# Gated cross-attention block: evictions of the VO stage shared out, exponentials of the first softmax spread, sums of the first attention reordered

## The chip, the core and the metric

The kernel runs on one core of a Trainium2 chip. The core has five engines that run side by side, each with its own in-order queue: TensorE (PE in the profile, with PEld for its weight loads) multiplies matrices into PSUM banks; VectorE (DVE) and ScalarE (ACT) work elementwise and can read PSUM; GpSimd (POOL) works elementwise on SBUF; SyncE (SP) issues DMAs. An instruction starts when those before it in its queue are issued and the semaphores that it waits for have been raised. The metric is the device time of one execution in microseconds (us), of which several runs are taken; the profiler's span is from the first to the last instruction of one execution.

## The reference, cut to what matters

All data is float32: `x` is (4, 2048, 512), the context (4, 77, 384), 16 heads of 64, a softmax over 77 keys.

```python
def attention(x, context, Wq, Wk, Wv, Wo, bo):
    q, k, v = split_heads(x @ Wq), split_heads(context @ Wk), split_heads(context @ Wv)
    attn = softmax(einsum('bhid,bhjd->bhij', q, k) * 64 ** -0.5)
    return merge_heads(einsum('bhij,bhjd->bhid', attn, v)) @ Wo + bo

def ffn(x, W, b, logits, u):                      # one of 8 weight matrices, by a gumbel draw
    idx = argmax(log_softmax(logits) - log(-log(u)))
    return x @ W[idx] + b[idx]

x = x + tanh(g_xattn) * attention(layernorm(x), ctx_768, Wq, Wk, Wv, Wo, bo)
x = x + tanh(g_ffn) * ffn(layernorm(x), W, b, logits, u)
```

## The kernel before

**Folded weights.** The queries and the output projection are folded into the small context once per batch: M = Wq K^T, so that scores are `x M`, and VO = V Wo for each head, so that attention's output is `P VO`. The keys are padded to 80 and laid out as ten chunks of 128 rows (8 keys of each of the 16 heads); `tgx`, the gate tanh(g_xattn), is multiplied into VO when it leaves PSUM.

**Groups.** The 8192 tokens are worked in 16 groups of 512. For each group `i` there are three products: scores (`ps_s`), attention (`ps_a`) and feed-forward (`ps_f`). Work of neighbouring groups is interleaved by hand: the schedule is the order of the Python statements (`tc.manual_schedule()`), and each engine runs its instructions in that order. Nothing is planned by costs.

**Seven products for eight.** Class `Seven` multiplies 2x2 blocks with seven block products (Strassen's method in Winograd's form). The sums of column blocks (T1 to T4, `Columns.sum`) and of weight blocks (`weight_sum`) are made on GpSimd ahead. The order of the steps is in `ORDER`: (weight block, column block, accumulator, opens a bank).

```python
ORDER = ((0, "B11", 0, True), (3, "T1", 1, True), (4, "T2", 0, False), (1, "B21", 2, True),
         (5, "T3", 0, False), (6, "B22", 1, False), (2, "T4", 0, False))
```

Accumulators are used again: steps 0, 2, 4 and 6 all add onto accumulator 0, and after each of them `post(s)` reads the running sum out of PSUM. So step 2 may start only when `post(0)` has read, step 4 after `post(2)`, step 6 after `post(4)`. `post` of steps 0, 1, 2 and 6 is a copy on ScalarE (L472, for attention with a bias at L476); `post` of steps 3, 4 and 5 is an addition on VectorE (L491). Weight sums: `weight_sum(w, 0)` makes block 5, 1 makes block 3, 2 makes block 4, 3 makes block 6 (L123). Attention's second step therefore needs `weight_sum(vo, 1)` and T1 of the probabilities, its third `weight_sum(vo, 2)` and T2. The scores of a group come as three `Seven`s: `s0` (two row blocks), `s1` (two) and `s2` (one); `s1` and `s2` run together in a loop of seven steps.

**Softmax of a group.** Scores are transposed on VectorE into the tile `s` (`s_rows`, L520), four heads' parts side by side (16 token slices each). `head_max` (VectorE, L529 and L531) gives a negative scaled maximum, `exps(i, a, b)` runs exponentials number a to b-1 out of 64 (ScalarE, L537, one for each token slice of a head part), `head_sum` adds rows and takes the reciprocal (VectorE, L544 and L545), `head_scale` multiplies (GpSimd, L548), and `p_columns(i, k0, k1)` transposes chunks k0 to k1-1 of the result into `pT` (VectorE, L557); each chunk takes a part of all four head parts. `pT` chunks 0 to 4 are the upper half and feed T1. The tile `s` exists once: the scores of the next group overwrite it.

**The stretch around the change** (L738 to L800) lies between the first group's scores and its attention. It holds the building of VO for head pairs 3 to 7 (`build_vo`: six matmuls into six banks, six evictions with the gate, L339 on VectorE or L341 on ScalarE as the letters of its argument say in turn, then four stores to DRAM), the scores of group 1, and the softmax of group 0. `load_vo(0)` fetches VO back in its blocked form after the last store. `centre_wf` and `weight_sum(wf, ..)` prepare the feed-forward weight on GpSimd. Seven PSUM banks rotate among all products. After that a loop over the groups begins at L802; in its first pass (i = 1) attention of group 0 runs beside the softmax of group 1, with T2, T3, T4 of the probabilities and `weight_sum(vo, 3)` on GpSimd, and then the feed-forward of group 0, whose T1 is made on GpSimd from attention's last residuals (L924 to L929).

Of the kernel before, what the change touches and what calls it, by code (L numbers as in the profile page):

```python
# [19 lines left out]
def flamingo_block_kernel(  # L20
# [34 lines left out]
    NT, D = x.shape  # L55
# [32 lines left out]
    def bank(name):  # L88
        return pm.tile([P, 512], F32, tag="mm", name=name)
# [8 lines left out]
    vo = cp.tile([P, 7, KH, D // 2], F32, tag="vo")  # L98
# [8 lines left out]
    def pieces(t, at, n):  # L107

        return [t[:, ds(at + e * n * T, n * T)].rearrange("p (n v t) -> p n v t", v=2, t=T2) for e in range(2)]
# [4 lines left out]
    def flat(t):  # L114
        n = len(t.shape) - 1
        names = " ".join("abcdef"[:n])
        return t.rearrange(f"p {names} -> p ({names})")

    def weight_sum(w, n, engine=None):

        to, a, b_, op = ((5, 0, 3, ALU.subtract), (3, 3, 2, ALU.add), (4, 3, 0, ALU.subtract),
                         (6, 1, 4, ALU.subtract))[n]
        (engine or nc.gpsimd).tensor_tensor(flat(w[:, to]), flat(w[:, a]), flat(w[:, b_]), op)  # L123
# [65 lines left out]
    def by_chunk(t):  # L189

        return t.rearrange("p (a q e) -> p q a e", a=NA, e=32)

    def chunked(t):
        return t.rearrange("p (q a e) -> p q a e", a=NA, e=32)
# [61 lines left out]
    def v_cols(p, at, n):  # L256
        return vT_f[:, ds(p * BP + at, n)] if p < 7 else wf_f[:, ds(6 * D + at, n)]
# [65 lines left out]
    def stage_of(h):  # L323

        return vo_st[h if h < 2 else 2 + (h - 2) % (len(vo_st) - 2)]

    def build_vo(p, engines):
        n = 0
        for c in range(3):
            r = min(P, BP - c * P)  # L330
            for hh in range(2):
                stg = stage_of(2 * p + hh)
                hr = ts(hh, DH)
                ps = bank("ps_vo")

                nc.tensor.matmul(ps, v_cols(p, c * P, P)[hr], wo[hr, p, :], start=True, stop=True)  # L336
                src, dst = by_chunk(ps[:r, :]), chunked(stg[:r, c, :])
                if engines[n % len(engines)] == "D":
                    nc.vector.tensor_scalar(dst, src, tgx[:r], None, ALU.mult)  # L339
                else:  # L340
                    nc.scalar.activation(dst, src, AF.Copy, scale=tgx[:r])  # L341
                n += 1
        for hh in range(2):
            d, stg = vo_d[2 * p + hh], stage_of(2 * p + hh)
            nc.sync.dma_start(out=d[0 : 2 * P].rearrange("(c r) e -> r c e", r=P), in_=stg[:, 0:2])
            nc.sync.dma_start(out=d[2 * P :], in_=stg[: BP - 2 * P, 2])
# [5 lines left out]
    def load_vo(bi):  # L352
        src = vo_d.rearrange("h (r b k) e -> (h r) b k e", b=B, k=NK)[:, bi]
        for o, c in ((0, 0), (1, 0), (1, 1), (0, 1)):
            nc.sync.dma_start(out=vo[:, BLK[o, c]], in_=src[:, ts(c, KH), ts(o, D // 2)])
# [63 lines left out]
    def key_chunk(t, k):  # L419

        return t.rearrange("p h g j -> p g h j")[:, :, :, ts(k, R)]
# [95 lines left out]
    def s_rows(i, k, cols):  # L517
        if i not in sc:
            sc[i] = wp.tile([P, HA, NG, JP], F32, tag="s", name="s")
        nc.vector.transpose(key_chunk(sc[i], k), cols.rearrange("p (g h r) -> p g h r", h=HA, r=R))  # L520

    def head(i, h):
        return sc[i][:, h, :, :J]
# [3 lines left out]
    def head_max(i, h):  # L527
        mx = stat[:, ds((16 + h) * NG, NG)]
        nc.vector.tensor_reduce(mx, head(i, h), AX.X, ALU.max)  # L529
        nmx[h] = small.tile([P, NG], F32, tag=f"nmx{h}", name="nmx")  # L530
        nc.vector.tensor_tensor(nmx[h], mx, norms[i].down, ALU.mult)  # L531

    def exps(i, n0, n1):

        for n in range(n0, n1):
            h, g = n // NG, n % NG
            nc.scalar.activation(head(i, h)[:, g, :], head(i, h)[:, g, :], AF.Exp,  # L537
                                 scale=norms[i].up[:, g : g + 1], bias=nmx[h][:, g : g + 1])
# [3 lines left out]
    def head_sum(i, h):  # L542
        sums[h] = sm = small.tile([P, NG], F32, tag=f"sm{h}", name="sm")
        nc.vector.tensor_reduce(sm, head(i, h), AX.X, ALU.add)  # L544
        nc.vector.reciprocal(sm, sm)  # L545

    def head_scale(i, h):
        nc.gpsimd.tensor_tensor(head(i, h), head(i, h), sums[h].unsqueeze(2).to_broadcast([P, NG, J]),  # L548
                                ALU.mult)

    def p_columns(i, k0, k1):
        for k in range(k0, k1):
            if k == 0:
                t = wp.tile([P, NK * T + KH * T2], F32, tag="pT", name="pT")
                pT[i] = Columns(t[:, : NK * T].rearrange("p (n t) -> p n t", t=T),
                                T1=t[:, NK * T :].rearrange("p (n t) -> p n t", t=T2))
            nc.vector.transpose(pT[i].all[:, k, :].rearrange("p (g h r) -> p g h r", h=HA, r=R),  # L557
                                key_chunk(sc[i], k))
# [103 lines left out]
    def centre_wf(wfr, c):  # L662
        nc.gpsimd.tensor_tensor(wfr[:, c, :], wfr[:, c, :], wf_mean, ALU.subtract)
        for o in range(2):
            nc.gpsimd.tensor_scalar(chunked(wf[:, BLK[o, c // 2], c % 2, :]), by_chunk(wfr[:, c, :])[:, ts(o, 2)],
                                    tgf, None, ALU.mult)
# [10 lines left out]
    def norm_step(n, s):  # L677
        if s == 0:
            n.gather()
        elif s == 1:  # L680
            n.calc()
            n.power()
        elif s == 2:
            n.back()
# [11 lines left out]
    s1 = Seven("ps_s", w_scores, xc[0], (2, 3), SNAP)  # L696
# [27 lines left out]
    s2 = Seven("ps_s", w_scores, xc[0], (4,), SNAP1)  # L724
# [15 lines left out]
    s1 = Seven("ps_s", w_scores, xc[1], (2, 3), pieces(spare, 0, 2))  # L740
    s2 = Seven("ps_s", w_scores, xc[1], (4,), SNAP1)
    head_max(0, 0)
    build_vo(3, "AAD")
    head_max(0, 1)
    exps(0, 0, 8)
    e = (8, 16, 24, 32, 41, 50, 57)
    for s in range(6):
        s0.product(s)
        s0.post(s)
        if s < 2:  # L750
            centre_wf(wfr, 2 * s)
            centre_wf(wfr, 2 * s + 1)
        if s == 2:
            weight_sum(wf, 0)
            weight_sum(wf, 1)
        if s == 3:
            weight_sum(wf, 2)
        if s < 4:
            build_vo(4 + s, "DDA" if s < 2 else "D")
        if s < 2:  # L760
            head_max(0, 2 + s)
        exps(0, e[s], e[s + 1])
        if s == 3:
            weight_sum(wf, 3)
            load_vo(0)
        if 3 <= s:
            head_sum(0, s - 3)
            head_scale(0, s - 3)
    exps(0, 57, 64)
    for s in range(7):  # L770
        s1.product(s)
        s2.product(s)
        if s == 0:
            s1.post(0)
            s2.post(0)
            s0.product(6)
            s0.post(6)
            head_sum(0, 3)
            head_scale(0, 3)
        if s == 3:  # L780
            norm_step(n1, 2)
        if 1 <= s < 5:
            p_columns(0, (0, 2, 5, 7)[s - 1], (2, 5, 7, 10)[s - 1])
        if s == 2:
            pT[0].sum("T1")
        if s == 3:
            weight_sum(vo, 0)
        if s == 4:
            weight_sum(vo, 1)
        if s == 5:  # L790
            weight_sum(vo, 2)
            for k in range(4):
                s_rows(1, (0, 1, KH, KH + 1)[k], s0.chunk(k // 2, k % 2))
        if 0 < s:
            s1.post(s)
            s2.post(s)
    for sv, k0, nk in ((s1, 2, 2), (s2, 4, 1)):
        for half in range(2):
            for k in range(nk):
# [2 lines left out]
    for i in range(1, NGRP):  # L802
# [4 lines left out]
        if 1 < i:  # L807
# [27 lines left out]
            s1 = Seven("ps_s", w_scores, xc[i], (2, 3), SNAP)  # L835
            s2 = Seven("ps_s", w_scores, xc[i], (4,), SNAP1)
# [35 lines left out]
        for s in range(7):  # L872
# [12 lines left out]
            if 1 <= s:  # L885
                e = (0, 10, 20, 32, 44, 56, 64)
# [225 lines left out]
```

## Time and profile before

| | us |
|---|---|
| median of 3 runs | 1246.3 (1245.36 to 1249.04) |
| the profiled execution: device time | 1246.03 |
| the profiled execution: span | 1244.2 |
| TensorE busy in it | 1234.0 (99%) |
| VectorE, GpSimd, ScalarE busy | 907.3 (73%), 895.4 (72%), 683.4 (55%) |
| VO pairs 3 to 7 with five score steps | 89.30 to 111.66 |
| the other score steps of group 1 | 111.66 to 135.17 |
| attention of group 0 | 135.17 to 165.39 |

The granted clock of TensorE was 0.998. Times in the profile count from the start of the span. A timeline row gives start, duration, engine, line, operation, output and inputs, shape and count of a run of like instructions, and in brackets the idle time ahead and what ended it. The chain that ended last is followed back from the last instruction; its rows give start, duration and what ran. In the waits, the columns are the total, the count and the longest wait.

### The profile page before, as it was taken

To read this page: it belongs to the slowest core of one execution; us is meant where nothing else is said; L and a number is where in the kernel's file an instruction comes from. 1 tells how busy PE (TensorE), PEld (TensorE's weight loads), DVE (VectorE), ACT (ScalarE), POOL (GpSimd) and SP (SyncE) were. 2 spreads that over 40 slices of the span, in tenths; PEclk is the share of its full clock that TensorE was granted. 3 is DMA by queue.
4 is the path that set the end of the run, shared out by engine and by line. 5 is a ranking of instruction groups with operands and counts; after the bars stand their busy time and mean duration, and the time that the engine had idled before them with its cause. 6 is when DMAs were issued, how large, how long until landed. Compare 5 with 4: busy or idle time off the path is not lost.

```text
span 1244.2 us, 16997 instructions
## 1 busy us (share of the span) xinstructions
PE 1234.0 (99%) x5704; PEld 1063.7 (85%) x5704; DVE 907.3 (73%) x1850; ACT 683.4 (55%) x1957; POOL 895.4 (72%) x486
## 2 busy tenths in 40 slices
PE   9999999999999999999999999999999999999997
PEld 6686888888888888888888888888888888888886
DVE  6778976666977766677776767776776877666576
ACT  4639545638274563827356382745638274563824
POOL 5558885857957785685968778575976877585766
PEclk9999999999999999999999999999999999999999
DMA  9868200314024030304106030212304121010102
GB/s 268 300 203 274 57 1 1 68 43 111 1 50 103 1 68 1 68 22 112 20 1 153 1 68 2 47 22 85 68 1 111 43 51 18 1 35 1 35 1 67
DMA packets 95221, 80.27 MB, mean 65 GB/s; under 512 B 3856, under 2 KB 83088, under 8 KB 95136
## 3 DMA queue, kind: packets, MB, share of 16 engines
q1 hardware_dynamic: 92496, 76.61, 24.1%
q10 hardware_dynamic: 2032, 1.47, 0.4%
q8 instruction: 45, 0.74, 0.3%
q0 software_dynamic: 608, 1.13, 0.2%
q14 instruction: 40, 0.33, 0.1%
HBM read 44.07 MB, written 35.13 MB: 64 GB/s over the span
## 4 chain that ended last, share of the span: by engine, by line
PE 96%; DVE 2%; ACT 0%; POOL 0%; issue 0%; DVEq 0%
PE ps_s L466 39%; PE ps_a L466 37%; PE ps_f L466 15%; PE ps_kv L270 2%; PE ps_vo L336 2%; PE ps_m L300 1%; DVE s L370 1%; PE ps_w L167 0%; ACT t L591 0%; POOL r L398 0%; DVE t L417 0%; DVE r L393 0%; DVE y L417 0%; DVE snap L491 0%; DVE y L587 0%
## 5 line engine op out<-in xcount | busy, mean ns | idle before, releaser
L466 PE MATMUL ps_a<-pT,vo 128*128 128x256 f32 x2240 | 486.2, 379 | 0.0
L466 PEld LDWEIGHTS ps_a<-pT,vo 128*128 128x128 f32 x2240 | 425.6, 190 | 57.9
L537 ACT ACTIVATE s<-s,nmx,up 128x77 f32<-128x77 f32 x1024 | 355.6, 445 | 0.8 <-DVE nmx L531 0.8
L437 POOL TENSOR_TENSOR pT<-pT 128x1280 f32<-128x1280 f32 x64 | 186.0, 2907 | 171.4 <-PE ps_a L466 161.9
L466 PE MATMUL ps_s<-tq,m 128*128 128x256 f32 x1280 | 290.6, 380 | 0.0
L466 PEld LDWEIGHTS ps_s<-tq,m 128*128 128x128 f32 x1280 | 242.6, 190 | 36.1 <-issue 2.3
L472 ACT COPY snap<-ps_s 128x512 f32<-128x512 f32 (+1 forms) x188 | 93.6, 515 | 292.7 <-DVE t L417 130.5
L466 PE MATMUL ps_s<-xc,m 128*128 128x256 f32 x960 | 221.1, 379 | 0.0
L466 PEld LDWEIGHTS ps_s<-xc,m 128*128 128x128 f32 x960 | 182.2, 190 | 27.3 <-issue 1.2
L548 POOL TENSOR_TENSOR s<-s,sm 128x1232 f32<-128x1232 f32 x64 | 145.2, 2271 | 46.7 <-DVE sm L545 46.7
L491 DVE TENSOR_TENSOR snap<-snap,ps_s 128x512 f32<-128x512 f32 (+1 forms) x141 | 83.7, 594 | 130.1 <-PE ps_s L466 125.0
L466 PE MATMUL ps_f<-tq,wf 128*128 128x256 f32 x512 | 118.3, 379 | 0.0
L557 DVE STREAM_TRANSPOSE pT<-s 128x512 f32<-128x512 f32 x160 | 101.0, 678 | 15.6 <-POOL s L548 15.6
L437 POOL TENSOR_TENSOR tq<-xc,tq 128x512 f32<-128x512 f32 x64 | 85.4, 1335 | 35.5 <-PE ps_f L466 33.0
L398 POOL TENSOR_TENSOR r<-r,neghalf 32x16 f32<-32x16 f32 (+1 forms) x33 | 93.2, 2833 | 21.9 <-DVE r L393 21.3
L466 PEld LDWEIGHTS ps_f<-tq,wf 128*128 128x128 f32 x512 | 97.3, 190 | 13.2
L544 DVE TENSOR_REDUCE sm<-s 128x16 f32<-128x1232 f32 x64 | 91.5, 1430 | 20.7 <-ACT s L537 20.7
L520 DVE STREAM_TRANSPOSE s<-snap 128x512 f32<-128x512 f32 x156 | 99.9, 685 | 6.1 <-ACT snap L472 3.8
L529 DVE TENSOR_REDUCE ps_st<-s 128x16 f32<-128x1232 f32 x64 | 92.4, 1444 | 2.1
L466 PE MATMUL ps_f<-xc,wf 128*128 128x256 f32 x384 | 90.7, 379 | 0.0
L437 POOL TENSOR_TENSOR tq<-xc 128x512 f32<-128x512 f32 x64 | 81.6, 1275 | 7.1 <-DVE xc L412 5.8
L472 ACT COPY snap<-ps_f 128x512 f32<-128x512 f32 x63 | 36.9, 586 | 87.8 <-PE ps_f L466 85.2
(138 smaller groups left out, 1187.0 us busy)
## 6 DMA issues: line engine op xcount, KB each, us to landing
xg<-in_x_dram SPq DMA_DIRECT2D x64, 256.0 KB, 6.0
out_dram<-y SPq DMA_DIRECT2D x60, 256.0 KB, 4.1
vo<-vo_d SPq DMA_DIRECT2D x16, 640.0 KB, 6.4
m<-m_d SPq DMA_DIRECT2D x12, 640.0 KB, 4.2
vo_d<-vo SPq DMA_DIRECT2D x14, 512.0 KB, 3.3
m_d<-vo SPq DMA_DIRECT2D x4, 960.0 KB, 5.0
wq<-in_WqT_dram SPq DMA_DIRECT2D x8, 256.0 KB, 6.5
wq<-in_Wo_dram SPq DMA_DIRECT2D x1, 2048.0 KB, 13.8
```

Of the source, the lines that this page charges most:

```text
L270: nc.tensor.matmul(ps[:, :n], w[:, c, ts(p, P)], keys[:, c].rearrange("p b j -> p (b j)"), start=(c == 0), stop=(c == NCC - 1))
L398: nc.gpsimd.tensor_tensor(r, r, neghalf[:32, : r.shape[1]], ALU.pow)
L437: (engine or nc.gpsimd).tensor_tensor(self.at[name], self.at[a], self.at[b_], op)
L466: nc.tensor.matmul(self.ps[r][:, n, :], self.w(blk, c, pair), self.cols(cname, c), start=(first and n == 0 and c == 0), stop=(c == h - 1), ...
L472: nc.scalar.copy(dst, self.ps[r])
L491: nc.vector.tensor_tensor(c, c, self.ps[r], ALU.add)
L520: nc.vector.transpose(key_chunk(sc[i], k), cols.rearrange("p (g h r) -> p g h r", h=HA, r=R))
L529: nc.vector.tensor_reduce(mx, head(i, h), AX.X, ALU.max)
L537: nc.scalar.activation(head(i, h)[:, g, :], head(i, h)[:, g, :], AF.Exp, scale=norms[i].up[:, g : g + 1], bias=nmx[h][:, g : g + 1])
L544: nc.vector.tensor_reduce(sm, head(i, h), AX.X, ALU.add)
L548: nc.gpsimd.tensor_tensor(head(i, h), head(i, h), sums[h].unsqueeze(2).to_broadcast([P, NG, J]), ALU.mult)
L557: nc.vector.transpose(pT[i].all[:, k, :].rearrange("p (g h r) -> p g h r", h=HA, r=R), key_chunk(sc[i], k))
```

## The change

The change touches only the order and the engine of instructions; what is computed stays the same.

- `build_vo` of pairs 4 to 7 takes the letters `ADD` (ScalarE, VectorE, VectorE in turn) in place of `DDA` for pairs 4 and 5 and `D` for pairs 6 and 7.
- Six exponentials in place of eight run before the loop over the `s0` steps, five to seven instead of seven to nine in each step, four after it; the last sixteen move into steps 0 to 3 of the `s1`/`s2` loop, four in each.
- `head_sum` and `head_scale` of head part 0 stay at `s0` step 3, part 1 moves to step 5, part 2 to step 0 and part 3 to step 3 of the next loop.
- `weight_sum(vo, 0)` moves up to step 0, ahead of the last scaling; `weight_sum(vo, 1)` stays at step 4, now just behind T1 of `pT`, which moves from step 2 to step 4.
- The transposes into `pT` move from steps 1 to 4 (2, 3, 2, 3 of them) to steps 3, 4 and 5 (3, 3, 4).
- `post` of the `s1`/`s2` steps moves from the end of a step to its beginning, ahead of exponentials, sums and transposes of that step.

```diff
-    exps(0, 0, 8)
-    e = (8, 16, 24, 32, 41, 50, 57)
+    exps(0, 0, 6)
+    e = (6, 13, 20, 27, 34, 39, 44)
     for s in range(6):
         s0.product(s)
         s0.post(s)
...
         if s < 4:
-            build_vo(4 + s, "DDA" if s < 2 else "D")
+            build_vo(4 + s, "ADD")
         if s < 2:
             head_max(0, 2 + s)
         exps(0, e[s], e[s + 1])
         if s == 3:
             weight_sum(wf, 3)
             load_vo(0)
-        if 3 <= s:
-            head_sum(0, s - 3)
-            head_scale(0, s - 3)
-    exps(0, 57, 64)
+        if s in (3, 5):
+            head_sum(0, s // 2 - 1)
+            head_scale(0, s // 2 - 1)
+    exps(0, 44, 48)
     for s in range(7):
         s1.product(s)
         s2.product(s)
...
             s2.post(0)
             s0.product(6)
             s0.post(6)
+        else:
+            s1.post(s)
+            s2.post(s)
+        if s < 4:
+            exps(0, 48 + 4 * s, 52 + 4 * s)
+        if s == 0:
+            head_sum(0, 2)
+            head_scale(0, 2)
+            weight_sum(vo, 0)
+        if s == 3:
             head_sum(0, 3)
             head_scale(0, 3)
-        if s == 3:
             norm_step(n1, 2)
-        if 1 <= s < 5:
-            p_columns(0, (0, 2, 5, 7)[s - 1], (2, 5, 7, 10)[s - 1])
-        if s == 2:
+            p_columns(0, 0, 3)
+        if s == 4:
+            p_columns(0, 3, 6)
             pT[0].sum("T1")
-        if s == 3:
-            weight_sum(vo, 0)
-        if s == 4:
             weight_sum(vo, 1)
         if s == 5:
+            p_columns(0, 6, 10)
             weight_sum(vo, 2)
             for k in range(4):
                 s_rows(1, (0, 1, KH, KH + 1)[k], s0.chunk(k // 2, k % 2))
-        if 0 < s:
-            s1.post(s)
-            s2.post(s)
```

## The prediction

> **What bounds the kernel now.** I read the summary first, then the chain that ended last in order of time, then the waits of the weight loads, then the timelines of ScalarE, VectorE and GpSimd between 90 and 170 us.
>
> ```profile
> span 1244.2 us, 16997 instructions
> PE 1234.0 (99%) x5704; PEld 1063.7 (85%) x5704; DVE 907.3 (73%) x1850; ACT 683.4 (55%) x1957; POOL 895.4 (72%) x486
> PE 96%; DVE 2%; ACT 0%; POOL 0%; issue 0%; DVEq 0%
> ```
>
> TensorE carries 96% of the chain. A microsecond that another engine loses is free until TensorE waits for it, and then it is lost for good, because nothing later is idle enough to win it back. The chain around the change (start, duration, what):
>
> ```profile
> 94.00 2.77 PE ps_vo L336 x12
> 96.78 1.92 PE ps_s L466 x8
> 98.70 3.02 PE ps_vo L336 x12
> 101.72 1.92 PE ps_s L466 x8
> 103.64 3.08 PE ps_vo L336 x12
> 106.72 1.92 PE ps_s L466 x8
> 108.64 3.02 PE ps_vo L336 x12
> 111.66 23.51 PE ps_s L466 x108
> 135.17 30.22 PE ps_a L466 x140
> 165.39 10.36 PE ps_f L466 x48
> ```
>
> VO pair 4 takes 2.77 us, pairs 5, 6 and 7 take 3.02, 3.08 and 3.02. From 111.66 on every product has its steady length (1.73 us for two pairs of 2x2 blocks, so 2.59 for one step of the two remaining score products together, 4.32 for attention): no waits. The waits agree: the last line is the only one of size that a faster eviction could take away.
>
> ```profile
> PEld ps_vo L336 <- issue: 7.6, 30, 0.3
> PEld ps_vo L336 <- DVE vo L339: 0.9, 4, 0.2
> ```
>
> The helpers are just in time. On ScalarE, VectorE and GpSimd (start, duration):
>
> ```profile
> 106.04 13.83 ACT L537 ACTIVATE s<-s,nmx,up 128x77 f32<-128x77 f32 x40
> 115.53 8.95 POOL L548 TENSOR_TENSOR s<-s,sm 128x1232 f32<-128x1232 f32 x4 [2.45 <-DVE sm L545]
> 124.51 4.27 DVE L557 STREAM_TRANSPOSE pT<-s 128x512 f32<-128x512 f32 x7 [2.89 <-POOL s L548]
> 131.01 8.87 POOL L123 TENSOR_TENSOR vo<-vo 128x1280 f32<-128x1280 f32 x3
> 139.31 1.44 DVE L529 TENSOR_REDUCE ps_st<-s 128x16 f32<-128x1232 f32 x1
> 164.60 1.27 POOL L437 TENSOR_TENSOR tq<-xc 128x512 f32<-128x512 f32 x1
> ```
>
> The first softmax's last exponential ends at 119.7, its last scaling at 124.5, the transposes into pT follow, and GpSimd's sums of VO blocks run till 139.9, when attention's second product (135.17 + 4.32 = 139.5) is about to use them. The last row is the first feed-forward sum: ready at 165.87, used at 165.39 + 1.73 = 167.12. Margin 1.25 us.
>
> **The change, part by part.**
>
> *Evictions.* Pairs 4 to 7 now go A D D A D D. VectorE loses two evictions in each of pairs 6 and 7, ScalarE wins them (pairs 4 and 5 keep two and four, in another order). Gain: the excess over 2.77 us, 0.25 + 0.31 + 0.25 = **0.81 us**, and no more, since 2.77 is a pair's length where no eviction is late. The excess also tells when a bank runs out: VectorE's first two evictions of pair 6 end at about 105.5 and 106.2 (104.79 and 0.67 apart, 0.74 each), and a sixth product that waits for the second of them, due at 103.64 + 0.2 + 5 x 0.43 = 106.0, gives 0.2 to 0.3. So a pair finds four or five banks free. In pair 4 the first eviction now stands on ScalarE behind six exponentials. They begin at 94.11 and cost 0.346 each (13.83 us for 40), the score eviction after them 0.48: it runs from 96.65 to 97.35, where VectorE began it at 95.09. The sixth product is due at 94.00 + 0.2 + 2.15 = 96.35. If it takes that bank it waits 1.1 us; if another is free, nothing. I take **1.1**, because by the count above five are free there at most. In pairs 5 to 7 ScalarE is free when the pair starts. Net +0.3: a step that was at 115.3 is at 115.6.
>
> *A table rule.* ScalarE alternates Copy evictions with exponentials in both versions, and the trace has one table load of 1.28 us in this stretch, before the first exponential, and none after the Copy groups at 97.33 and 101.68: by that row the price is 0. The Trainium skill, "ScalarE: Activation LUTs", section "Rules for kernel authors", says to group by table set before switching, and its section "What ACT_TABLE_LOAD costs" puts a switch at 2.66 us; by that, some five new alternations of two switches would be an estimated 27 us of ScalarE time. The same page, section "Table sets", has Copy in every set, as the trace shows.
>
> *Exponentials.* Before, 40 run without a break to 119.7. Now 27 to 47 run after pair 7's last ScalarE eviction (about 111.8), 21 x 0.346 = 7.3, till 119.1. The other sixteen go four by four behind the evictions of score steps 0 to 3, which wait for TensorE. Steps 0 to 6 start at 115.6, 119.9, 122.5, 125.1, 127.7, 130.3 and 132.9 (2.59 apart, the first score group's last product, 1.73, after step 0). Evictions of step 0 and of that product till 120.6, four exponentials till 122.0; step 1's evictions till 123.0, four till 124.35; step 2's till 125.55, eight till **128.35**. The last exponential is 8.6 us later.
>
> *Sums, scalings, transposes.* VectorE's row sum of the last head with its reciprocal takes 1.7 us (119.90 to 121.62): till 130.1. GpSimd's scaling takes 2.27: till 132.4. The first VO sum, moved ahead of it, waits for VO's load (issued at 117.43, median 6.4 us, so about 124) and ends by 127: it lies in GpSimd's idle time till 130.1, uncovered if the load lands past 127. VectorE, in order, stands at its first transposes from about 128.5 to 132.4, but for the row sum. **Behind them in its queue are the evictions of step 4**, and step 6's products add onto the accumulators that those read. Three transposes (0.61 each) till 134.3, the eviction 0.65: 134.95. Step 6 is due at 132.87. First stall **2.15 us** with the semaphore; attention starts at 137.6.
>
> *Second stall.* The other eviction (0.33) and two more transposes end at 136.5 and release GpSimd's T1 sum (2.92): 139.4. The second VO sum (2.95) now stands behind it: 142.4. Attention's second product uses it and is due at 141.9: **0.5 us**. Then the third VO sum till 145.3 and T2 till 148.2; the third product is due at 146.7: **1.5 us**. Attention ends at 165.39 + 0.3 + 2.15 + 0.5 + 1.5 = 169.85.
>
> *Third stall.* VectorE after 132.4 has ten transposes, four step evictions and ten row transposes of the second scores, 14.0 us: till 146.4, where before it was 139.3. So the second softmax starts 7.1 us late, against 4.45 of TensorE. First maximum till 148.1; on ScalarE ten exponentials and an attention eviction (0.72) till 152.3, ten and one till 156.5 (the fifth product adds onto what this one reads, at 156.8: just in time), 28 to the end of head 2 till 166.2. Row sum till 167.9, scaling till 170.1, residual 1.28, feed-forward T1 1.29: 172.75. Its product is due at 169.85 + 1.73 = 171.6: **1.2 us**. The next sums follow 1.25 apart for products of 1.73, and VectorE's pause of 1.52 us at 184 takes up its lag. Nothing comes back.
>
> SP issues the same DMAs in the same order; the stores of pairs 6 and 7 and the load behind them move with the evictions, within the microsecond or two that the load has.
>
> Sum: -0.81 + 1.1 + 2.15 + 0.5 + 1.5 + 1.2 = **+5.65 us**. The profiled execution took 1246.03 us (span 1244.2 and 1.8 around it), 0.3 below the runs' median of 1246.3. So 1251.7 against the first, 1251.95 against the second: I say **1251.8**. With pair 4's other end, 1250.7.
>
> **The rivals.** About 0.3% (3.7 us, so 1250.0) is what a measurement of this kernel can tell from no change.
>
> *Not slower: the exponentials come in time.* Every stall hangs on the last exponential, microsecond for microsecond, since the scaling, the transposes, GpSimd's sums and the second softmax follow it in order. It decides at 126.4: from 1.95 us earlier than I walk it, the time is under 1250; at 125.7, 1249.1. For it: 16 exponentials are only 5.5 us of ScalarE, and it has idle time. Against it: ScalarE's own work from 111.8, with no wait for TensorE at all, is 37 x 0.346 and 2.8 of evictions, so 127.4.
>
> *Hidden: no stall at all.* If step 4's evictions ended by 132.9 and T2 by 144, only the evictions' effect would be left, between -0.81 and +0.3: 1245.5 to 1246.6. The program's order puts three transposes, and the scaling that they wait for, ahead of those evictions; against it by 2.15 us. This bounds the fast side: nothing here gives over 0.81 us.
>
> *ScalarE late in every VO pair.* The first eviction of each pair is now ScalarE's, behind seven exponentials (2.4 us). If each of the pairs 5, 6 and 7 waits like pair 4, 3.3 us more: 1255.1. Against it: a step lasts 4.7 us and holds 2.4 + 1.2 + 0.5 of ScalarE's work. Half of it, 1253.4.
>
> **How the numbers follow.** Forecast 0.70 (own range 1250.1 to 1253.0: pair 4's wait, and half a microsecond of each chain of sums); exponentials in time 0.15 (1248.5 to 1250.0); hidden 0.04; ScalarE late in VO 0.11 (1253 to 1255). The range 1249.0 to 1253.6 leaves out the hidden case, a part of the case before it and most of the last. Slower by over 0.3%: 0.70 + 0.11, less 0.02 for the edge at 1250.0: 0.79. Faster 0.01, within 0.3% 0.20.
>
> **What would show it.** Pair 4 longer than 2.77 us with ScalarE's eviction as releaser, pairs 5 to 7 at 2.77; the first softmax's last exponential at 128; VectorE idle until the scaling at 132; step 6 of the scores late by 2 us; attention's second and third products waiting for GpSimd's VO and T2 sums; the first feed-forward sum behind its product; every later stage as before, 5 to 6 us on. I am wrong if attention starts before 136, if the feed-forward shows no wait, or if the load lands past 127 (each microsecond more adds one).

## The result, and the profile after

The changed kernel takes 1252.34 us (median of 6 runs, 1251.82 to 1252.88) against 1245.83 (6 runs of the kernel before, 1245.2 to 1249.04): ratio 1.0049, 95% interval 1.0039 to 1.0059. That is 6.5 us slower; 1251.8 and +5.65 were predicted. The profiled execution took 1252.06 us, its span is 1250.3, its granted clock 0.999.

The chain that ended last, for the stretch of the change (start, duration, what):

```profile
96.22 0.59 ACT vo L341
96.95 1.97 PE ps_s L466 x8
98.92 3.08 PE ps_vo L336 x12
102.00 1.92 PE ps_s L466 x8
103.93 3.00 PE ps_vo L336 x12
106.93 1.93 PE ps_s L466 x8
108.85 2.95 PE ps_vo L336 x12
111.81 13.16 PE ps_s L466 x60
124.99 0.37 ACT snap L472
125.36 2.75 ACT s L537 x8
128.14 1.45 DVE sm L544
...
130.01 2.27 POOL s L548
132.31 1.90 DVE pT L557 x3
...
140.24 6.06 DVE s L520 x10
146.32 1.46 DVE ps_st L529
...
166.18 1.45 DVE sm L544
...
168.04 2.27 POOL s L548
...
171.62 1.28 POOL tq L437
...
172.94 8.90 PE ps_f L466 x40
```

Before, this chain was TensorE alone from the first VO pair on. Now it leaves TensorE at 125, goes through ScalarE, VectorE, GpSimd and the second softmax, and comes back at 172.94, with the feed-forward's second product: TensorE does not wait all that time, but its waits in it are what this chain dictates. TensorE's own timeline names each place where it stood; the bracket gives its idle time and the releaser:

```profile
96.95 1.97 PE L466 MATMUL ps_s<-tq,m 128*128 128x256 f32 x8 [0.69 <-ACT vo L341]
134.83 2.86 PE L466 MATMUL ps_s<-tq,m 128*128 128x256 f32 x12 [2.11 <-DVE sn L491]
142.25 4.58 PE L466 MATMUL ps_a<-pT,vo 128*128 128x256 f32 x20 [0.24 <-POOL vo L123]
148.10 21.85 PE L466 MATMUL ps_a<-pT,vo 128*128 128x256 f32 x100 [1.27 <-POOL pT L437]
172.94 3.29 PE L466 MATMUL ps_f<-tq,wf 128*128 128x256 f32 x14 [1.26 <-POOL tq L437]
```

Step 6 of the scores, attention's second and third products and the feed-forward's second are the four places that the prediction walked to, with the releasers that it named. A time lost is the distance between starts, a little more than the idle time in the bracket. From VO pair 4 to the scores after VO TensorE took 17.66 us before and 18.32 now (+0.66); from there to attention 23.42 and 25.78 (+2.36); attention 30.21 and 32.27 (+2.06); from the feed-forward's start to the next group's second score product 13.82 and 15.34 (+1.52). Together +6.6; the span grew by 6.1, because this execution reached VO pair 4 0.5 us sooner. All later groups have the old length of 72.5 us.

### The profile page after: what moved, and what is told of

Its sections match the earlier page's. It is cut to its first block, busy times and chain, and to the rows that moved or that the text cites. A ratio compares the mean times of both kernels' runs of the same rounds, so it can differ in the third digit from the quotient of the medians.

```text
span 1250.3 us, 16998 instructions
## 1 busy us (share of the span) xinstructions
PE 1234.4 (99%) x5704; PEld 1064.2 (85%) x5704; DVE 905.1 (72%) x1846; ACT 685.5 (55%) x1961; POOL 894.9 (72%) x486
## 4 chain that ended last, share of the span: by engine, by line
PE 92%; DVE 4%; ACT 3%; POOL 1%; issue 0%; DVEq 0%; ACTq 0%; POOLq 0%
PE ps_s L466 38%; PE ps_a L466 34%; PE ps_f L466 14%; PE ps_kv L270 2%; ACT s L537 2%; PE ps_m L300 1%; PE ps_vo L336 1%; DVE s L370 1%; DVE pT L557 0%; DVE s L520 0%; ACT t L591 0%; POOL s L548 0%; PE ps_w L167 0%; DVE snap L491 0%; POOL r L398 0%
```

## The experiments

A whole run scatters by a microsecond or more, so the runs are compared by a distance inside their profiles too: on TensorE's timeline, from the first product of VO pair 3 to the feed-forward's first product with a T1 sum. It holds all that the change touches. Each distance comes from one execution and so has no interval of its own; the untouched step from VO pair 3 to pair 4 takes 4.70 or 4.71 us in all twelve profiles. Before: 89.23 to 166.95, 77.72 us. Changed: 88.72 to 172.94, 84.22 us, **+6.50**.

| kernel | from, to (us) | against before | median, ratio (95%) |
|---|---|---|---|
| changed | 88.72, 172.94 | +6.50 | 1252.34, 1.0049 (1.0039 to 1.0059) |
| order of sums alone | 88.90, 172.32 | +5.70 | 1251.74, 1.0046 (1.003 to 1.0063) |
| evictions alone | 89.44, 170.94 | +3.78 | 1249.84, 1.0031 (1.0021 to 1.0041) |
| changed, evictions as before | 91.75, 175.33 | +5.86 | 1251.78, 1.0043 (1.0026 to 1.006) |
| changed, exponentials 6, 6, 4 | 88.71, 172.78 | +6.35 | 1251.91, 1.0045 (1.0028 to 1.0062) |
| order of sums, last row sum ahead | 89.20, 169.40 | +2.48 | 1248.48, 1.0019 (1.0009 to 1.0028) |
| changed, transposes behind | 88.61, 171.91 | +5.58 | 1251.24, 1.0044 (1.0027 to 1.006) |
| changed, VO sum early | 89.19, 173.43 | +6.52 | 1252.78, 1.0053 (1.0036 to 1.0069) |
| changed, both of these | 88.78, 172.30 | +5.80 | 1251.92, 1.0057 (1.004 to 1.0073) |
| before, half evictions | 89.58, 166.54 | -0.76 | 1245.61 (one run) |
| before, one eviction more on ScalarE | 89.19, 167.81 | +0.90 | 1246.41, 1.0005 (0.9995 to 1.0015) |

**Which gate? The order of sums alone.** The prediction hung every stall on the last exponential. The rival puts the blame on the place of the last row sum in VectorE's queue. This kernel has the new order of sums in both loops, with the old exponentials and evictions (edit against the changed kernel):

```diff
-    exps(0, 0, 6)
-    e = (6, 13, 20, 27, 34, 39, 44)
+    exps(0, 0, 8)
+    e = (8, 16, 24, 32, 41, 50, 57)
...
-            build_vo(4 + s, "ADD")
+            build_vo(4 + s, "DDA" if s < 2 else "D")
...
-    exps(0, 44, 48)
+    exps(0, 57, 64)
...
-        if s < 4:
-            exps(0, 48 + 4 * s, 52 + 4 * s)
```

> The kernel before with the new order of sums, scalings, transposes and evictions of the score steps alone; evictions of VO and the exponentials stay as they were, so the last exponential ends at 119.7 us. Theory E (the prediction's: every stall hangs on the last exponential, microsecond for microsecond): the last row sum can start 8 us earlier than in the changed kernel, the stalls go, within 0.5 us of before. Theory Q (place in the queue): the last row sum now stands on VectorE behind the evictions of score step 3, which wait for TensorE till about 127.5 whatever ScalarE does; it starts there as in the changed kernel, and the time is before + 5.2 us (stalls of 2, 0.5, 1.5 and 1.25), ratio 1.0042.

Measured: +5.70. ScalarE's last exponentials on its timeline:

```profile
105.70 13.83 ACT L537 ACTIVATE s<-s,nmx,up 128x77 f32<-128x77 f32 x40
```

and VectorE's timeline around the last row sum:

```profile
126.31 0.69 DVE L491 TENSOR_TENSOR sn<-sn,ps_s 128x512 f32<-128x512 f32 x1 [6.89 <-PE ps_s L466]
127.17 0.42 DVE L491 TENSOR_TENSOR snap<-snap,ps_s 128x256 f32<-128x256 f32 x1 [0.18 <-PE ps_s L466]
127.51 1.43 DVE L544 TENSOR_REDUCE sm<-s 128x16 f32<-128x1232 f32 x1
```

The exponentials are done at 119.5. VectorE then idles 6.89 us, because the next in its queue is step 3's eviction, and the row sum that could run stands behind it. So an early last exponential does not take the delay away: the place in the queue is enough to cause it. The predicted step, in which the exponential alone decides, is refuted, and 5.7 of the 6.5 us come with the order of sums alone.

TensorE pays in other places than in the changed kernel. Its timeline at step 6:

```profile
134.20 4.54 PE L466 MATMUL ps_s<-tq,m 128*128 128x256 f32 x12 [1.96 <-DVE sn L491]
```

After the wait these twelve products take 4.38 us, up to attention's start at 138.58, in place of 2.59: the granted clock fell to 0.50 (see the last section). Attention then loses 0.35 us in place of 2.06, and the feed-forward's second product still waits 1.29 us for GpSimd's T1 sum.

**Less of the exponentials' delay.** In the changed kernel the two gates meet: the last exponential ends at 128.11, step 3's evictions on VectorE at 128.07.

```profile
125.26 2.85 ACT L537 ACTIVATE s<-s,nmx,up 128x77 f32<-128x77 f32 x8
...
127.65 0.42 DVE L491 TENSOR_TENSOR snap<-snap,ps_s 128x256 f32<-128x256 f32 x1 [0.18 <-PE ps_s L466]
```

This run moves one of them.

```diff
-        if s < 4:
-            exps(0, 48 + 4 * s, 52 + 4 * s)
+        if s < 3:
+            exps(0, 48 + 6 * s, min(54 + 6 * s, 64))
```

> The changed kernel with its last sixteen exponentials six, six and four in score steps 0, 1 and 2 in place of four in each of steps 0 to 3: the last one ends about 0.7 us earlier (127.4). Theory E (stalls hang on the last exponential): 0.7 us less than the changed kernel. Theory Q (the row sum stands behind step 3's evictions on VectorE, which end at 128.06): the row sum starts at the same 128.1 and the time falls by 0.0 to 0.3 us.

Measured: the last exponential ends at 127.37, the row sum starts at 127.98 instead of 128.14, the distance falls by 0.15 us. The other 0.6 us by which the exponential is earlier bring nothing: the queue holds the row sum. The reverse, late exponentials with the row sum ahead of the evictions, was not run; by the rows above the row sum would then still wait for the exponential till 128.11. So in the changed kernel either gate alone holds the row sum till about 128.

**The row sum ahead of the evictions.** If the place in the queue is the cause, moving the row sum (with its scaling and a small normalisation step) must bring time back, in the kernel where its data are ready early (edit against the run with the order of sums alone):

```diff
             weight_sum(vo, 0)
-        if s == 3:
+        if s == 2:
             head_sum(0, 3)
             head_scale(0, 3)
             norm_step(n1, 2)
+        if s == 3:
             p_columns(0, 0, 3)
```

> The run with the new order of sums alone (exponentials and VO evictions as before), but the last row sum and scaling moved from step 3 to step 2, so that on VectorE they stand ahead of step 3's evictions; the transposes stay. Theory Q: the row sum starts when the last exponential is done, 120 us; the scaling then waits only for the first VO sum on GpSimd (126 to 128.5) and the transposes start 3 us earlier: no stall in the scores, one of 1.0 us at attention's third product and one of 1.25 at the feed-forward, before + 2.2 us instead of + 6. If the transposes' own place behind step 3's evictions were the cause, nothing would change: before + 6.

Measured: +2.48 in place of +5.70. VectorE's timeline:

```profile
119.86 1.44 DVE L544 TENSOR_REDUCE sm<-s 128x16 f32<-128x1232 f32 x1
...
128.75 1.90 DVE L557 STREAM_TRANSPOSE pT<-s 128x512 f32<-128x512 f32 x3 [0.85 <-POOL s L548]
```

GpSimd's:

```profile
123.59 2.90 POOL L123 TENSOR_TENSOR vo<-vo 128x1280 f32<-128x1280 f32 x1 [0.81 <-issue]
126.45 2.27 POOL L548 TENSOR_TENSOR s<-s,sm 128x1232 f32<-128x1232 f32 x1
```

The row sum starts at 119.86, as before the change. So the place of the row sum is worth 3.2 of the 5.7 us. The rest is places in queues too, of two kinds that no run here separates. GpSimd is free for the scaling at 122.8, but the scaling stands behind the first VO sum and starts at 126.45. And the transposes themselves stand on VectorE behind step 3's evictions, which end at 127.9 (127.48 + 0.42); for the scaling they wait only 0.85 us more. TensorE waits only at attention's third product (0.75 us idle) and at the feed-forward (1.29).

**The evictions alone**, in the kernel before:

```diff
-            build_vo(4 + s, "DDA" if s < 2 else "D")
+            build_vo(4 + s, "ADD")
```

> The kernel before with the letters ADD for pairs 4 to 7 and nothing else. By the prediction's account of the evictions alone: -0.81 to +1.1, at most 1.001 times before. Rival (ScalarE is full): with eight exponentials ahead, pair 4's first eviction is 0.7 us later than in the changed kernel and TensorE waits about 2.0 us there; four more evictions (0.58 us each) push the last exponential from 119.7 to about 124, the evictions of score step 0 stand behind it, step 2 adds onto what they read and waits 1.3 us, and step 6 another 0.8: before + 3.7 us, ratio 1.0030.

Measured: +3.78; ScalarE is full. Its last exponentials on its timeline:

```profile
113.46 11.05 ACT L537 ACTIVATE s<-s,nmx,up 128x77 f32<-128x77 f32 x32
```

and TensorE's timeline at its waits:

```profile
98.36 1.97 PE L466 MATMUL ps_s<-tq,m 128*128 128x256 f32 x8 [1.37 <-ACT vo L341]
...
125.03 2.86 PE L466 MATMUL ps_s<-tq,m 128*128 128x256 f32 x12 [0.64 <-ACT sn L472]
136.31 2.86 PE L466 MATMUL ps_s<-tq,m 128*128 128x256 f32 x12 [0.65 <-DVE sn L491]
```

The exponentials end at 124.5 instead of 119.9, and score step 0's eviction, which step 2 needs, stands behind them. TensorE idles 1.37, 0.64 and 0.65 us where 2.0, 1.3 and 0.8 were expected; of the rest, pairs 5 and 6 take 0.62 us (3.43 and 3.28 from start to start in place of 3.02 and 3.07), and most of what is left lies around the three waits, where the starts are further apart than the idle time says. In the changed kernel the same evictions go with exponentials that are spread between the score steps, and step 2 does not wait.

**The changed kernel with the old evictions** (the same line, the other way round):

> The changed kernel with the VO evictions of before (DDA for pairs 4 and 5, D for 6 and 7). Prediction's account of the evictions: they cost 0.3 us net in the changed kernel, so 0.3 less; measured in its profile they cost 0.66, so 0.66 less, all of it at pair 4 (TensorE's 0.69 us wait ends). Later stalls as in the changed kernel. If the evictions and the sums shared one delay, more would come back, up to the 4.1 us that the evictions cost alone.

Measured: 0.64 us less than the changed kernel, 0.66 expected from its profile. So the parts are: order of sums +5.70; the exponentials' spread, which this run has in addition, +0.16; the new evictions on top +0.64. The parts add up only in this order: alone, on the kernel before, the evictions cost 3.78.

**One eviction only.** How much room had ScalarE before?

```diff
-            build_vo(4 + s, "DDA" if s < 2 else "D")
+            build_vo(4 + s, "DDA" if s < 2 else "D" if s == 2 else "DADDDD")
```

> The kernel before with one eviction of VO pair 7 (the second) moved from VectorE to ScalarE. If ScalarE had room: pair 7 loses its 0.25 us, the time is the same or 0.25 us less. If ScalarE is full up to the evictions of score step 0: the exponentials that are left end 0.6 to 1.6 us later than 119.7, step 2 of the scores waits about 0.4 us for ScalarE's eviction and step 6 about 0.8 for VectorE's, and the time is before + 1.0.

Measured: +0.90 in the stretch, 1.0005 (0.9995 to 1.0015) as a whole, too little to be told from no change by time alone. The one wait in the stretch that is not there before is step 6's for VectorE, 0.64 us idle. The 0.4 us expected at step 2 did not show in the profile. ScalarE had no room in this stretch before the change: from 94 to 120 it was busy 25.99 of 26.00 us.

**Do the stalls add up?** In the prediction the total is a sum of stalls. First, in the changed kernel, the stall of score step 6 is taken away:

```diff
         if s == 3:
             head_sum(0, 3)
             head_scale(0, 3)
             norm_step(n1, 2)
-            p_columns(0, 0, 3)
         if s == 4:
-            p_columns(0, 3, 6)
+            p_columns(0, 0, 6)
```

> The changed kernel with its first three transposes into pT moved from step 3 to step 4, behind that step's two evictions on VectorE. Theory of one chain: step 6 of the scores no longer waits (2.1 us less), but everything after hangs on the transposes, which only gain the 0.9 us of the two evictions: attention's second product waits 1.8 in place of 0.5, and the time falls by 0.9 us against the changed kernel (before + 5.6). Theory of separate stalls that add up: it falls by 2.1 to 2.4 us (before + 4.2).

The stall of 2.11 us is gone and the distance falls by 0.92. TensorE's timeline shows where the rest went, to attention's second product, which idled 0.24 us in the changed kernel:

```profile
141.19 4.58 PE L466 MATMUL ps_a<-pT,vo 128*128 128x256 f32 x20 [1.67 <-POOL vo L123]
147.03 21.85 PE L466 MATMUL ps_a<-pT,vo 128*128 128x256 f32 x100 [1.25 <-POOL pT L437]
171.91 3.72 PE L466 MATMUL ps_f<-tq,wf 128*128 128x256 f32 x16 [1.31 <-POOL tq L437]
```

Second, the stalls of attention are taken away, by letting GpSimd make the second VO sum while it idles:

```diff
         if s == 3:
+            weight_sum(vo, 1)
             head_sum(0, 3)
...
             pT[0].sum("T1")
-            weight_sum(vo, 1)
```

> The changed kernel with the second VO sum moved ahead of GpSimd's last scaling, into 3.9 us in which GpSimd idles. Attention's second and third products then find their sums ready: their waits, together 2.06 us in the changed kernel, go. Theory of separate stalls: 2.06 us less. Theory of one chain: the second softmax still starts at 146.3, so attention's fifth product waits for ScalarE's eviction instead (about 1.7 us), the feed-forward's second for its T1 sum (1.5), and the time is the changed kernel's within 0.3 us.

Measured: +6.52, 0.02 from the changed kernel. Attention's second and third products no longer wait; the fifth does, and the feed-forward:

```profile
135.32 2.86 PE L466 MATMUL ps_s<-tq,m 128*128 128x256 f32 x12 [2.12 <-DVE sn L491]
...
157.20 13.19 PE L466 MATMUL ps_a<-pT,vo 128*128 128x256 f32 x60 [1.75 <-ACT snap L476]
...
173.43 3.72 PE L466 MATMUL ps_f<-tq,wf 128*128 128x256 f32 x16 [1.32 <-POOL tq L437]
```

Both together:

> The changed kernel with both moves at once: the first three transposes behind step 4's evictions, the second VO sum ahead of the last scaling. The waits of score step 6 (2.1 us) and of attention's second and third products (2.06) go, but for about 0.4 us. Theory of separate stalls: about 4 us less, before + 2.5. Theory of one chain, which the two single moves support: attention's fifth product waits about 2.7 us for ScalarE's eviction, the feed-forward 1.5, and the time falls by the 0.9 us of the transposes alone: before + 5.6.

Measured: +5.80, 0.70 less than the changed kernel (0.9 expected), though about 4 us of stalls are gone from where they were. TensorE now idles 2.68 us at attention's fifth product, for ScalarE:

```profile
155.86 14.88 PE L466 MATMUL ps_a<-pT,vo 128*128 128x256 f32 x60 [2.68 <-ACT snap L476]
```

The feed-forward's wait of 1.5 us that was expected did not come, because TensorE itself is late there: after the 2.68 us the clock fell to 0.50 again, and these 60 products take 14.71 us in place of 12.95. The T1 sum was ready at 172.05 and its product began at 172.30, so about 0.2 us of the time that did not come back is the clock's. The stalls are not separate losses. They are one chain's lateness, paid in instalments wherever TensorE first meets it.

**What holds VO pairs 5 to 7 at 3 us?** The change was to win back 0.81 us there and won 0.09: the pairs are 3.08, 3.00 and 2.95 us long. In the kernel before, the evictions of pairs 5 to 7 are now halved, which leaves out half of VO for their heads:

```diff
                 src, dst = by_chunk(ps[:r, :]), chunked(stg[:r, c, :])
+                if p >= 5:
+                    src, dst = src[:, :2], dst[:, :2]
```

> The kernel before, with the evictions of VO pairs 5, 6 and 7 cut to half of their columns (the other half of VO is left as it was, so those heads' output is left out in part): each takes about 0.45 us in place of 0.74. If the excess of these pairs over 2.77 us (0.25, 0.31, 0.25) is a wait for a bank that an eviction has not freed, it goes: 2.77 to 2.80 each. If it has another source, it stays at 3.0.

The distances from each pair's start to the next score product become those of an unstalled pair (rows on TensorE's timeline, where a row runs 0.08 us past the next start):

```profile
98.97 2.85 PE L336 MATMUL ps_vo<-wq 64*128 64x512 f32 x12
103.67 2.88 PE L336 MATMUL ps_vo<-wq 64*128 64x512 f32 x12
108.41 2.85 PE L336 MATMUL ps_vo<-wq,wf 64*128 64x512 f32 x12
```

So the excess is a wait for evictions. It goes when each is shorter (0.48 us here on either engine), and stays when VectorE merely has fewer of them: a whole eviction takes 0.69 us on ScalarE and 0.74 on VectorE, and in the changed kernel pair 6's first two start at 105.07 and 105.12, side by side, without the pair getting shorter by more than 0.1. Which bank is the late one was not measured. The -0.76 us is also close to a bound: with the three pairs at the length of an unstalled one, their evictions have nothing more to give. None of the runs that compute everything beats the kernel before, and nothing in them points to one that would by a measurable amount.

## Why the prediction was right, and where it was not

**The total and the stages.** 1251.8 was said, 1252.34 measured. By stage: evictions +0.3 said, +0.66 measured; score step 6 2.15 and 2.36; attention's two waits 2.0 and 2.06; feed-forward 1.2 and 1.52. Together that is 5.65 said (the terms as printed add up to 5.64) and 6.60 measured, every stage a little too low. The total comes out nearer than that partly by luck: it was counted from about 1246.15 us, and the kernel before has a median of 1245.83 over the six runs.

**Evictions: two terms mis-sized, in opposite directions.** The gain of 0.81 us was 0.09: the step that failed took an excess that comes with late evictions for one that goes when VectorE has fewer of them. The half evictions show that it goes when they get shorter. Pair 4's wait of 1.1 us was 0.75 with its semaphore (0.69 idle). The releaser was the eviction that was named, but it met the score product after the pair, not the pair's sixth product, which did not wait: the count of free banks was one too low there.

**The last exponential: a step that was only half of the cause.** Its time was right (128.35 said, 128.11 measured), and so was that of the row sum (128.4 and 128.14). But the rival "the exponentials come in time", with its point of decision at 126.4, and the sentence that every stall follows the last exponential microsecond for microsecond, are refuted: with the exponentials done at 119.5 the delay is 5.70 us. Step 3's evictions, which stand ahead of the row sum on VectorE, are missing from that step of the walk; I had seen that VectorE is in order for step 4's evictions, and not for step 3's. That the time was right all the same is luck: in this kernel the two gates open within 0.05 us of each other. Where two gates open together, a walk that names one gives the right time and half of the cause, and only moving them one at a time tells. (A small misreading beside it: before the change the last exponential ends at 106.04 + 13.83 = 119.87, not at 119.7.)

**The sum of stalls.** Each stall's term was near its measured size, and the sum came within a microsecond, because each was worked out from the delay that the ones ahead had left over. Taken as prices they mislead: the 2.36 us at step 6 and the 2.06 at attention, taken away, brought 0.92 and nothing.

**Rivals.** "ScalarE late in every VO pair" did not come: pairs 5 to 7 are together 0.09 us shorter than they were. The load of VO landed in time: the first VO sum ran from 123.17 to 126.07, 3.93 us before GpSimd's next work. Nothing came back after 185 us, as said: the groups that follow have their old length. ScalarE's alternation of copies and exponentials cost nothing, as read from the profile before: in this stretch the changed kernel too has one table load, 1.28 us at 92.30.

## What to carry to other kernels

Ask of every instruction that feeds a chain not only when its data are ready but what stands ahead of it in its own queue: in the run with the order of sums alone, a row sum whose input was ready at 119.5 waited till 127.5 behind an eviction that waited for TensorE. Put work that waits for a slow producer behind work that is ready, on each engine. And before mending a stall, follow its chain to the end: the lateness that is taken away in one place turns up at the next wait unless the start of the chain moves.

## What was not expected of the hardware

On ScalarE the room that the whole profile seems to show was not there. Before the change it is busy 55% of the span, but 25.99 of the 26.00 us from 94 to 120. One eviction more (0.69 us) in this stretch cost 0.90 us, and four more in pairs 6 and 7, with pair 4's and 5's in another order, cost 3.78.

TensorE's granted clock is 1.00 all through the stretch in the kernel before and the changed one (0.998 and 0.999 over the whole span), so it has no part in the +6.5 us that their profiles show. In three other runs a wait was followed by a granted clock of 0.50 for about 3.4 us (an estimate from slices of 1 us): at step 6 of the scores with the order of sums alone and with the exponentials 6, 6, 4, after 1.96 us idle in both, and in attention with both moves together, after 2.68 us. TensorE lost 1.79 us by it each time at step 6 and 1.76 in attention. Waits of 2.11 and 2.12 us at step 6, in the changed kernel and with the VO sum early, brought no such fall, so the length of the wait alone does not decide; what does was not found. In the changed kernel's other five runs, which were not profiled, the mean clock is 0.996 or 0.997, so it may have fallen there too; their times lie close around the profiled one. In the first two of the three runs the loss is hidden, since the feed-forward still waits there for GpSimd (1.29 and 1.28 us); in the third it is the 0.2 us named above.
